# A decoder's mixture-of-experts layer: inputs of six experts by scatter, fetch and transpose, and the first expert started one batch at a time

## The chip, the cores and the metric

The kernel runs on one core of a Trainium2 chip. A core has five engines that run their own instruction queues in order and wait for each other on semaphores: TensorE (PE, matrix products and transposes into PSUM), VectorE (DVE), ScalarE (ACT), GpSimd (POOL) and SyncE (SP, which here only issues DMAs; ACT and POOL issue some too). The metric is the device time of one execution in microseconds; the time before is the median of three runs.

## The reference

The input x is 2 batches of 1024 tokens of 256 features, in fp32. Six sublayers are added to it in turn, each on a layer norm of x: a linear attention with a feed-forward, a cross attention of text to x, a recurrent cell, a causal attention, a cross attention of x to 2 x 64 text rows with 16 heads, and last a mixture of 8 experts. The last two are what matters here:

```python
x = inputs.reshape(G, S, Mm)                       # 8 groups of 256 tokens, 256 features
logits = jnp.einsum('GSM,ME->GSE', x, router_w)    # 8 experts
dispatch, combine = _gating_top2(logits, C)        # two experts a token, C = 64 places per group and expert
expert_inputs = jnp.einsum('GSEC,GSM->EGCM', dispatch, x)
layer_w0 = jnp.einsum('EGCM,EMH->EGCH', expert_inputs, w0_kernel)   # H = 1368
layer_w1 = jnp.einsum('EGCM,EMH->EGCH', expert_inputs, w1_kernel)
hidden = jax.nn.gelu(layer_w0, approximate=True) * layer_w1
expert_outputs = jnp.einsum('EGCH,EHM->EGCM', hidden, wo_kernel)
out = jnp.einsum('EGCM,GSEC->GSM', expert_outputs, combine)
```

A token whose place in an expert is 64 or more is dropped there. `dispatch` is 0 or 1, so `expert_inputs` only moves rows of x to places; a place that no token has is a row of zeros.

## The kernel before

Tokens lie in SBUF as 16 tiles of 128 rows (tile t holds tokens 128t to 128t+127 of both batches in turn; two tiles are one group, four tiles are one *unit*, eight one batch). The layers run one after the other. The part that concerns us begins with the second cross attention, class `Cross`. It works on four units; each step is a small function (`norm`, `turn`, `proj`, `max`, `red`, `sc`, `exp`, `val`, `out`, `add` and so on), and the order of all steps of all units is written out by hand in the string `CROSS_ORDER` (line 1465). A step's name is followed by its unit and, for some, a half. `Cross.run` goes through the string and issues each step's instructions, so that each engine's queue has that order. Steps that begin with `route_` are pieces of `Experts.scores`: the layer norm of a unit into `xn` (L1928 to L183), the transpose by products with the identity (L1945), the router product (L1953). `choose` are the pieces of `Experts.choose`: for one batch, from the router's scores to two slots and two gates for each token; the place in the expert is a running count, made by products with a triangular matrix and with ones (L1992 to L2000). A slot is a row number of a table of expert rows: 512 (`AWAY`) + 512 per expert + the place, with 64 rows per group; 0 if the token was dropped. Units 0 to 2 and the choosing of batch 0 are in `CROSS_ORDER`. PSUM there is three banks of two (`s`) and two single ones (`t`).

`Experts.run_in` follows with two `s`, two `t` and two `o` banks. It has no order by hand at first; a scheduler places the instructions by their dependencies and by program order. Unit 3's scores and batch 1's choosing come first. Then the *dispatch*: for each tile, `dispatch` makes a one-hot matrix of 128 tokens x 512 places (8 experts x 64) with two DVE instructions (L2041, L2042); four such tiles were made in `CROSS_ORDER` (`ones`). PE multiplies it with the token rows (L2089), two tiles into one group, which gives the expert inputs with features on the partitions, as the next product needs them. ACT (L2098) and DVE (L2102) copy them to SBUF for all experts and groups.

Then the experts, one after the other. `hidden` has 11 chunks of up to 128 of the 1368 hidden features (`HCH`): four products of 512 columns for the two weights (L2149), gelu on ACT (L2157), a product on DVE (L2158). `outputs` has 44 products (matmuls) of 256 columns (L2164). Each fp32 matmul shows in the trace as two instructions. The rows of the first six experts (`MOST`) go to the table `eo_rows` in DRAM, on ACT's queue. After expert 5, `gather` fetches for each tile its two rows by an indirect DMA on POOL's queue (L2182, 32 of them) and adds them to x (L2176), while PE works on experts 6 and 7, whose outputs stay in SBUF and come back to the tokens by one product (`combine` makes its matrices, `last` applies them, L2195). Weights are loaded on SP's queue: `load(e + 2)` for w0 and w1 after expert e, with two buffers, and `load_out(e)` for the second weight, with one.

`Experts.constants` runs before the cross attention: number patterns by POOL, and zero rows into three parts of `eo_rows` on SP's queue. The weights' pool `wts`, in which `xn` lies, is closed by `held.close()` before the experts.

## Time and profile before

| what | value |
|---|---|
| median of three runs | 1771.98 us (1766.24 to 1774.56) |
| the profiled execution's own time | 1776.51 us |
| its span, first to last instruction | 1774.4 us |
| PE, DVE, ACT, POOL busy | 1677.3, 804.1, 512.7, 265.7 us |
| mean granted TensorE clock | 0.964 of full |
| first text product of the second cross attention | starts at 1158.37 us |
| end of its last output product (L1811) | 1257.98 us |
| first product of expert 0 | starts at 1305.69 us |
| one expert | 38.04 us hidden, 19.01 us outputs |
| dispatch products L2089 | 64 instructions, 30.7 us busy |
| expert weights to SBUF | 7.1 us from issue to landing, median |

How to read it: times in the trace are counted from the span's start. "Idle before" is time in which an engine did nothing ahead of an instruction, with what released it. The mean duration of a PE instruction overlaps its neighbours, so a run of them is best read from the starts. The granted clock is the share of TensorE's full clock that the throttle let through in a stretch of time.

### The profile page before, as it was taken

How to read it: one execution, taken by the hardware profiler on the slowest of the kernel's cores; microseconds unless marked ns; L12 is line 12 of the kernel's file. 1: busy time of each engine (PE TensorE's matmuls, PEld its weight loads, DVE VectorE, ACT ScalarE, POOL GpSimd, SP SyncE). 2: the span in 40 equal slices, each digit the busy share in tenths (PEclk: the TensorE clock that was granted, in tenths of full speed). 3: DMA queues.
4: the chain of work that ended last, by engine and by line, in shares of the span. 5: the costliest groups of instructions: out<-in, count | busy, mean ns of one | idle time of the engine just before them, and what ended most of it. 6: DMA issues, size and time to landing. Idle time of an engine off the chain costs nothing. (4 is left out here: it accounts for less than half of the span.)

```text
span 1774.4 us, 20965 instructions
## 1 busy us (share of the span) xinstructions
PE 1677.3 (95%) x8686; PEld 882.8 (50%) x8686; DVE 804.1 (45%) x1470; ACT 512.7 (29%) x870; POOL 265.7 (15%) x298
## 2 busy tenths in 40 slices
PE   6889899999999799989999999989899999999998
PEld 4655455343343446543433443456546645665566
DVE  5532224845653524467566667366641131111222
ACT  1221232233324132325555445533121111111110
POOL 2010131133213300203111111220000000000420
PEclk9889999999999899969999999999899999999999
DMA  5000000000000100000000000050003122322321
GB/s 225 1 3 1 0 1 4 1 0 1 1 1 1 36 1 0 31 1 1 1 1 1 1 1 1 1 195 2 1 0 107 69 74 71 107 92 81 100 68 48
DMA packets 30550, 59.16 MB, mean 33 GB/s; under 512 B 3640, under 2 KB 23672, under 8 KB 30072
## 3 DMA queue, kind: packets, MB, share of 16 engines
q1 hardware_dynamic: 25512, 50.46, 8.2%
q0 software_dynamic: 1536, 4.20, 0.9%
q10 hardware_dynamic: 3408, 3.17, 0.5%
q8 instruction: 69, 1.13, 0.3%
q14 instruction: 25, 0.20, 0.0%
HBM read 51.00 MB, written 6.82 MB: 33 GB/s over the span
## 5 line engine op out<-in xcount | busy, mean ns | idle before, releaser
L2149 PE MATMUL ps_s<-pair,w 128*128 128x512 f32 (+1 forms) x704 | 304.8, 592 | 0.2 <-ACT pair L2098 0.2
L2149 PEld LDWEIGHTS ps_s<-pair,w 128*128 128x128 f32 (+1 forms) x704 | 130.9, 187 | 164.4 <-issue 163.3
L1338 ACT ACTIVATE pT<-ps_t 128x512 f32<-128x512 f32 (+3 forms) x344 | 150.6, 490 | 149.5 <-PE ps_t L1303 147.7
L1228 PE MATMUL ps_s<-kT,qT 32*128 32x512 f32 (+3 forms) x768 | 182.1, 571 | 10.3 <-DVE part L1244 6.4
L1303 PE MATMUL ps_t<-qT,kT 32*128 32x512 f32 (+3 forms) x688 | 184.3, 554 | 2.2 <-ACT pT L1338 2.2
L2158 DVE TENSOR_TENSOR hid<-ga,ps_s 128x512 f32<-128x512 f32 (+1 forms) x88 | 60.5, 687 | 272.8 <-ACT ga L2157 272.8
L2164 PE MATMUL ps_o<-wo,hid 128*128 128x256 f32 (+1 forms) x704 | 153.5, 379 | 0.0
L1244 DVE TENSOR_REDUCE part<-ps_s 128x2 f32<-128x1024 f32 (+3 forms) x128 | 130.5, 1024 | 45.4 <-PE ps_t L1303 37.3
L2164 PEld LDWEIGHTS ps_o<-wo,hid 128*128 128x128 f32 (+1 forms) x704 | 133.8, 190 | 22.0 <-issue 4.1
L2157 ACT ACTIVATE ga<-ps_s 128x512 f32<-128x512 f32 (+1 forms) x88 | 52.5, 597 | 246.5 <-PE ps_s L2149 246.5
L1228 PEld LDWEIGHTS ps_s<-kT,qT 32*128 32x128 f32 x768 | 61.4, 194 | 86.8 <-issue 46.6
L1268 PE MATMUL ps_o<-pT,vr 128*32 128x256 f32 (+4 forms) x1408 | 99.5, 361 | 1.8 <-POOL pT L1296 1.5
L1296 POOL TENSOR_SCALAR_AFFINE_SELECT pT<-pT 128x256 f32<-128x256 f32 x128 | 51.9, 407 | 319.4 <-ACT pT L1338 310.3
L910 ACT ACTIVATE pT<-ps_s 128x1024 f32<-128x1024 f32 x64 | 65.5, 1023 | 115.4 <-PE ps_s L903 115.4
L2182 POOL DMA_INDIRECT found<-eo_rows,index x32 | 31.9, 997 | 422.5 <-DMA eo_rows<-rows 387.9
L798 DVE TENSOR_REDUCE part<-ps_s 128x2 f32<-128x1024 f32 x64 | 76.4, 1218 | 28.4 <-PE ps_s L791 27.7
L1236 DVE TENSOR_TENSOR ps_s<-ps_s,causal 128x256 f32<-128x256 f32 x128 | 54.9, 429 | 66.5 <-PE ps_t L1303 44.5
L915 POOL TENSOR_TENSOR acc<-acc,pT 128x1024 f32<-128x1024 f32 x24 | 59.4, 2476 | 160.0 <-ACT pT L910 157.3
L1268 PEld LDWEIGHTS ps_o<-pT,vr 128*32 128x32 f32 x1408 | 28.9, 109 | 98.4 <-issue 84.5
L1303 PEld LDWEIGHTS ps_t<-qT,kT 32*128 32x128 f32 x688 | 71.3, 191 | 12.1 <-ACT pT L1338 6.9
L791 PE MATMUL ps_s<-kT,qT 64*128 64x512 f32 x256 | 72.4, 646 | 0.6 <-DVE part L781 0.6
L830 PE MATMUL ps_o<-pT,vr 128*64 128x512 f32 x256 | 69.5, 624 | 0.0
(381 smaller groups left out, 2272.6 us busy)
## 6 DMA issues: line engine op xcount, KB each, us to landing
w<-in_w SPq DMA_DIRECT2D x32, 684.0 KB, 7.1
wo<-in_wo SPq DMA_DIRECT2D x8, 1280.0 KB, 6.9
eo_rows<-rows ACTq DMA_DIRECT2D x12, 256.0 KB, 4.5
w_ffn<-in_w_ffn SPq DMA_DIRECT2D x1, 2304.0 KB, 15.2
x<-in_x SPq DMA_DIRECT2D x4, 512.0 KB, 4.9
w<-in_w_cell SPq DMA_DIRECT2D x2, 1024.0 KB, 16.8
out_x<-x SPq DMA_DIRECT2D x8, 256.0 KB, 2.2
w<-in_w_lat SPq DMA_DIRECT2D x2, 768.0 KB, 16.8
```

Of the source, the lines that this page charges most:

```text
L791: nc.tensor.matmul(s3[:, hh, :], lhsT=q[rows, qt * P : (qt + 1) * P], rhs=kt[rows, half * 512 : (half + 1) * 512], start=True, stop=True,)
L798: nc.vector.tensor_reduce(part[:, half, qt, :], s3, AX.X, ALU.max, negate=True)
L830: nc.tensor.matmul(self.o[hh * 64 : hh * 64 + 64, :], lhsT=self.vr[b][:, kk, h * 64 : (h + 1) * 64], rhs=pT[:, hh, :], start=first, stop=last,
L910: nc.scalar.activation(pT, s3, AF.Exp)
L1228: nc.tensor.matmul(s3[:, hh, :n], lhsT=q[rows, qt * P : (qt + 1) * P], rhs=kt[rows, at : at + n], start=True, stop=True,)
L1244: nc.vector.tensor_reduce(out, s3[:, :, :n], AX.X, ALU.max, negate=True)
L1268: nc.tensor.matmul(self.o[hh * 32 : hh * 32 + 32, cols], lhsT=vr[:, kk, 4 * grp + hh, :], rhs=pts[hh // 2][:, hh % 2, cols], start=first, ...
L1303: nc.tensor.matmul(out, lhsT=kt[rows, kk * P : (kk + 1) * P], rhs=q[rows, j * 512 + q0 : (j + 1) * 512], start=True, stop=True,)
L1338: nc.scalar.activation(pT[:, hh, q0:], heads[hh][:, q0:], AF.Exp)
L2149: nc.tensor.matmul(s[:n, i * 512 : (i + 1) * 512], lhsT=wt[:, kc, at : at + n], rhs=v[:, kc, :], start=(kc == 0), stop=(kc == DC - 1),)
L2158: nc.vector.tensor_mul(hid[:n, hc, :], ga[:n], s[:n, 512:])
L2164: self.k.nc.tensor.matmul(o, lhsT=hid[:n, hc, st * P : (st + 1) * P], rhs=to[:n, hc, :], start=(hc == 0), stop=(hc == len(HCH) - 1),)
```

## The change

Experts 0 and 1 still get their inputs from PE, in one-hot matrices of 2 x 64 = 128 columns (`ones`, `disp`, `put`). The inputs of experts 2 to 7 are moved by DMA. `scatter` makes row numbers (a dropped token's slot 0 becomes a row of its own, its partition number) and issues 32 indirect DMAs on POOL's queue: each takes the 128 normalised rows of one tile to one of eight tables `xi_rows` in DRAM, one per group. `fetch(e)` reads expert e's places back with eight DMAs on POOL's queue, 64 rows each; `turned(e)` transposes them on PE (8 transposes) and copies them out on ACT. The tables are filled with zeros by eight more DMAs on SP's queue in `constants`; the zeros are the start of `xin`, the input buffer of experts 0 and 1.

Expert 0's hidden chunks are made in two halves, of 256 columns (one batch) each. `CROSS_ORDER` is a new order of the steps, and it now has all eight one-hots of batch 0, its two `disp` and two `put`. A second order by hand, `FIRST_ORDER`, lists what follows: expert 0's 11 chunks for batch 0 (`up`, `gelu`, `mul`, with the chunk as a hexadecimal digit), unit 3's scores, batch 1's choosing, one-hots and dispatch. After that come the scatter, batch 1's chunks of expert 0, and the fetches of experts 2 and 3. In the loop over experts, `turned(e + 1)` and `fetch(e + 3)` stand between the hidden chunks and the outputs. The pools are laid out anew: `wts` stays open to the end.

The core of the diff (the new orders shortened):

```diff
@@ CROSS_ORDER
-sum_3 ones_1 yT_2 val_3 inv_3 ones_3 spr_3 os_3 yT_3 out_2 ones_2 ones_0 out_3 add_2 route_stat_20
-route_stat_21 route_mean_2 route_root_2 add_3 route_norm_21 route_norm_20 route_turn_2 route_xT_2
-route_prod_2 route_copy_2
...
+choose_0 inv_2 spr_2 choose_0 val_2 choose_0 os_2 yT_2 choose_0 sc_30 choose_0 out_2 exp_30 ones_03
+ones_02 ones_01 ones_00 disp_00 add_2 route_stat_20 sum_3 put_00 ones_07 ones_06 ones_05 val_3 inv_3
+ones_04 spr_3 os_3 route_stat_21 disp_01 yT_3 route_mean_2 put_01 out_3 route_root_2 route_norm_20
+route_norm_21 add_3 route_turn_2 route_xT_2 route_prod_2 route_copy_2
@@
+FIRST_ORDER = """
+up_06 route_stat_30 up_08 gelu_06 route_stat_31 route_mean_3 mul_06 route_root_3 gelu_08 mul_08 up_04
+route_norm_30 route_norm_31 route_turn_3 gelu_04 mul_04 route_xT_3 route_prod_3 up_01 route_copy_3
+choose_1 choose_1 choose_1 gelu_01 choose_1 up_00 choose_1 mul_01 choose_1 gelu_00 mul_00 up_0a choose_1
+choose_1 up_05 gelu_0a ones_12 ones_13 up_07 gelu_05 ones_10 ones_11 mul_0a gelu_07 disp_10 mul_07
+mul_05 up_02 put_10 ones_15 ones_16 ones_14 up_09 gelu_02 ones_17 mul_02 disp_11 gelu_09 mul_09 up_03
+put_11 gelu_03 mul_03
+"""
@@ class Experts
-        self.iota = tile("iota", [P, E * C])
+        self.iota = tile("iota", [P, 2 * C])
+        self.iota1 = tile("iota1", [P, 2 * C])
...
+        self.xin = tile("xin", [P, 2, DC, G, C])
...
-        zero = tile("zero", [P, D])
+        zero = self.xin.rearrange("p e m g c -> p (e m g c)")[:, :D]
...
+        self.rows_in = [self.scratch.tile([AWAY + E * ROOM, D], F32, name=f"xi_rows{g}") for g in range(G)]
+        for g in range(G):
+            nc.sync.dma_start(
+                out=self.slots_of(g)[:, 2:, :], in_=zero[:C].unsqueeze(1).to_broadcast([C, E - 2, D])
+            )
...
-    def dispatch(self, t):
-        dm = self.pool.tile([P, E * C], F32, tag="dm", bufs=4, name="dm")
+    def ones(self, b, i):
+        nc, t = self.k.nc, b * TB + i
+        dm = self.ready[t] = self.pool.tile([P, 2 * C], F32, tag="dm", bufs=4, name="dm")
         s1, s2 = (slot[:, t : t + 1] for slot in self.slots)
         nc.vector.tensor_single_scalar(dm, self.iota, s1, op=ALU.is_equal)
         nc.vector.scalar_tensor_tensor(dm, self.iota, s2, dm, ALU.is_equal, ALU.add)
+    def disp(self, b, h):
+        tb = self.placed = self.k.t()
+        for g in range(2):
+            for mc in range(DC):
+                at = (g * DC + mc) * 2 * C
+                for half in range(2):
+                    t = b * TB + 4 * h + 2 * g + half
+                    self.k.nc.tensor.matmul(
+                        tb[:, at : at + 2 * C], lhsT=self.xn[:, t, mc * P : (mc + 1) * P], rhs=self.ready[t],
+                        start=(half == 0), stop=(half == 1),
+                    )
...
+    def scatter(self, pool):
...
+        for half in range(2):
+            for i in range(2):
+                for g in range(G):
+                    t = 2 * g + half
+                    nc.gpsimd.indirect_dma_start(
+                        self.rows_in[g], bass.IndirectOffsetOnAxis(ap=rows[i][:, t : t + 1], axis=0),
+                        self.xn[:, t, :], None,
+                    )
+    def fetch(self, e):
+        if e >= E:
+            return
+        xr = self.fetched[e] = self.hp.tile([P, G // 2, D], F32, tag="xr", bufs=2, name="xr")
+        for g in range(G):
+            h = g % 2 ^ (e == E - 1)
+            self.k.nc.gpsimd.dma_start(out=xr[h * C : (h + 1) * C, g // 2, :], in_=self.slots_of(g)[:, e, :])
+    def turned(self, e):
+        k, xr = self.k, self.fetched.pop(e)
+        s = k.s()
+        for kc in range(DC):
+            for i in range(4):
+                at = (kc * 4 + i) * P
+                k.nc.tensor.transpose(s[:, at : at + P], xr[:, i, kc * P : (kc + 1) * P], k.ident)
+        v = self.inputs[e] = self.hp.tile([P, DC, 512], F32, tag="xe", bufs=2, name="xe")
+        k.nc.scalar.copy(v, s.rearrange("p (c n) -> p c n", c=DC))
...
-    def run_in(self, pool, out, held):
...
+                    self.scatter(pool)
+                    for hc in range(len(HCH)):
+                        self.hidden(0, hc, 4 * C, 4 * C)
+                    self.fetch(2)
+                    self.fetch(3)
             for e in range(MOST):
-                for hid, to in hidden(e):
-                    pass
+                if e:
+                    self.begin(e)
+                    for hc in range(len(HCH)):
+                        self.hidden(e, hc)
+                if e:
+                    self.turned(e + 1)
+                    self.fetch(e + 3)
                 for sp in range(2):
```

For expert 7 the same `turned` stands after expert 6's hidden chunks.

## The prediction

> **What bounds the kernel now.** I read the busy times and the chain that ended last first, then the stretch that the change touches: as windows, as a piece of the chain, and on PE's own timeline.

> ```profile
> PE 1677.3 (95%) x8686; PEld 882.8 (50%) x8686; DVE 804.1 (45%) x1470; ACT 512.7 (29%) x870; POOL 265.7 (15%) x298
> PE 32%; DVE 2%; ACT 0%; issue 0%; POOL 0%; POOLq 0%; DVEq 0%; ACTq 0%
> ```

> TensorE (PE) is busy 95% of the span and carries the chain as far back as it is followed. So a saving is either PE work taken away or a PE gap filled. The windows, split at the end of the last cross-attention output product (1257.98), at the first product of expert 0 (1305.69), and at the ends of its two products (columns: length, busy time of PE, PEld, DVE, ACT, POOL, granted clock, DMA share, GB/s):

> ```profile
> 1158.37:1257.98 99.61, 90.34 (x985) 60.13 (x983) 70.96 (x168) 32.33 (x37) 13.61 (x9) 0.97 0.24 87
> 1257.98:1305.69 47.71, 40.80 (x130) 22.60 (x130) 28.51 (x92) 9.51 (x28) 1.87 (x2) 0.86 0.00 1
> 1305.69:1343.73 38.04, 38.03 (x89) 16.72 (x90) 8.49 (x18) 7.76 (x13) 0.00 (x0) 1.00 0.02 4
> 1343.73:1362.74 19.01, 19.01 (x90) 16.71 (x89) 1.38 (x2) 0.59 (x1) 0.00 (x0) 1.00 0.41 154
> ```

> The experts (rows three and four) are dense at full clock: there only work counts. Cross attention has 9.3 us of PE idle (99.61 - 90.34), the routing stretch 6.9 us, at a clock of 0.86. Its chain:

> ```profile
> 1258.00 1.22 DVE x L1821
> ...
> 1262.44 3.59 PE ps_t L1953 x16
> ...
> 1266.11 1.41 DVE r_st L1928 x4
> ...
> 1268.27 1.02 POOL rs_y L144
> ...
> 1269.87 0.45 PE ps_s L1945
> ...
> 1284.55 20.70 PE ps_s L2089 x48
> ...
> 1305.69 38.04 PE ps_s L2149 x88
> 1343.73 19.01 PE ps_o L2164 x88
> ```

> The reader is to see two things. PE waits up to 1269.87 on a chain of small steps (sum, statistics, root, normalisation); and then 48 dispatch instructions take 20.70 us, 0.431 us each, with nothing else to do. The trace shows two instructions per fp32 matmul.

> **The change, part by part**, against the profiled execution's own time (span 1774.4, 1776.5 with what lies around it; the median of the runs is 1772.0, 4.5 below, and I carry the difference over to the median).

> *Dispatch products narrowed.* Removed: 64 instructions of 512 columns, 64 x 0.431 = 27.6 us of PE, all on the path. Put in: 64 of 128 columns. By width that is 0.108 each; the routing product L1953 (8 columns) runs 16 in 1.88 us, 0.117 each, so the weight load is the floor: 64 x 0.117 = 7.5. **-20.1 us.** One-hot tiles fall on DVE from 16 x (0.475 + 0.749) to 16 x 2 x 0.337 (row of the 128x128 form), 19.6 to 10.8 us; the copies out fall from 24 ACT and 16 DVE to 8 ACT. Both engines have room, so this is worth nothing by itself but shortens the routing chain.

> *Transposes added.* Six experts x 8 of 128x128; L1945 runs 8 in 1.65 us: 6 x 1.65 = **+9.9 us**, all on PE, which has no gap there. Their copy (1.01 us on ACT, row of xT) lies under the 19.01 us of output products; their PSUM bank was released one 3.45 us step of products earlier (gelu 0.60 + product 0.69 after it): no wait. On PE the output products queue behind them; a late transfer would hold up those, and with them everything.

> *Expert 0 in two halves.* 88 instructions of 512 columns become 176 of 256: L2164 runs 88 of 256 in 19.01, 0.216 each, so 38.0 as before. Cost 0. But 11 steps of 1.73 us (19 us) now lie beside the routing.

> *Routing stretch.* I walk the new order with these rows' durations, T0 = end of the last cross output product, in us after T0. PE: transposes of tile group 2 to 1.7, copy awaited to 2.7, routing product to 4.6, two expert steps to 8.1. DVE: the statistics of group 3 (they wait, as L1928 does now, on the previous routing product, 4.6) to 6.1, root to 8.1, 7 combine pieces of 0.3 that stand in DVE's queue and two hidden products to 10.2, normalisation to 11.6. PE: third step to 10.3, **gap 1.3**, transposes to 13.3, **gap 1.1** (copy), routing product 16.5, steps and choosing to 25.5, **gap 1.6** (a PSUM bank freed by a product queued behind four one-hots), then steps and both dispatches to 38. Two extra activation-table loads (1.28 each on ACT) lie in it, one ahead of the exponential: 0.2 late. Then 11 steps of the second half: 57. Before: 1343.73 - 1257.98 = 85.75. Of the 28.75 less, 23.9 is dispatch (27.6 go, and of the new 7.5 half is left here, half now lies before T0); 4.9 is gaps and slow clock.

> *Clock.* PE does not always run at full rate after gaps:

> ```profile
> 1208.45 3.72 PE L1811 MATMUL ps_s<-w,yT 128*128 128x256 f32 x16
> 1217.92 5.38 PE L1811 MATMUL ps_s<-w,yT 128*128 128x256 f32 x16 [0.67 <-DVE yT L1803]
> ```

> The same 16 instructions cost 1.66 us more after gaps of 0.88 and 0.67. [...] by the row each cluster costs about 1.7. I take the row, once: 58.7, **-27.0** for the stretch. [...]

> *Cross attention reordered*, with two of the four dispatches and eight one-hots in it. The same walk from the first text product gives 103.5 against 99.6, that is 3.9 more, of which 3.8 are the two dispatches; but it has no slow clock, where now the clock of 0.97 costs 3 us, and a walk with no slack is about as much too slow. Bounds: +1 (dips gone) to +7 (dips on top). I take **+5**.

> *Scatter and fetch.* 32 indirect writes and 48 plain reads on POOL's queue, none in the trace of before. The nearest row is the gather at the end, issue after issue:

> ```profile
> 1657.17 1.20 POOL L2182 DMA_INDIRECT found<-eo_rows,index  x1 [387.90 <-DMA eo_rows<-rows]
> 1658.68 0.95 POOL L2182 DMA_INDIRECT found<-eo_rows,index  x1 [0.30 <-issue]
> 1659.93 0.95 POOL L2182 DMA_INDIRECT found<-eo_rows,index  x1 [0.30 <-issue]
> ```

> 1.25 us apart, 2.9 to landing, beside DVE's hidden products. Each scatter into one group's rows waits for the one eight issues (10 us) before: landed. The row numbers exist at T0 + 39; 32 scatters and the 8 reads of expert 2 make 40 x 1.25 + 2.9 = 53, ready at T0 + 92. Expert 2's transposes come after expert 0 (58.7), its outputs (19.0) and expert 1's products (38.0): T0 + 116. Slack 24 us, cost 0; from (116 - 39 - 2.9) / 40 = 1.85 us per issue it costs. [...] By the row, nothing. DVE's work there (hidden products with one operand in PSUM) is what ran beside the gather, so I take the row. Lower bound 0 too; no gain is possible here. Later reads have a whole expert (57 us) for 10 us of issues, and are ahead of the gather on POOL.

> *SP's queue* gets eight zero fills (3.1 MB) behind the expert weights, ahead of expert 0's second weights. The DMA engines are now busy to about 1183 at 365 GB/s; 8.6 us more is an estimate from that rate. The first writer of the memory that they read comes some 60 us later. Cost 0.

> **Sum.** Stretch -27.0, cross +5, transposes +9.9: **-12.1 us**. By the other account: dispatch -20.1, transposes +9.9, gaps and clock -2. Predicted median: 1772 - 12 = **1760**.

> **Rivals.**
> - *The gaps close* (22%). The 19 us of expert steps fill every wait, and the front-loaded normalisations of the cross stage leave it without dips: cross +1, stretch at its pure work of 31.6 + 19 + 2 = 53: -33. With +9.9: -22, **1750**. For it: a stretch with more PE work than chain. Against it: two PSUM banks, and DVE is in order.
> - *DVE keeps the routing late* (17%). One-hots, combine pieces and hidden products are in one queue; three waits more of 2 us and one more dip, and the cross stage at +7: -2, **1770**. For it: DVE is busy 71 of 99.6 us in the cross stage.
> - *POOL's transfers are late*, the slower side (8%). Place: PE before the transposes of expert 2. Price: 40 times what an issue exceeds 1.85 us. At 2.15 us it has eaten the gain; at 2.5 it is **1786**. Against it: the row above.
> - *The narrowing isn't worth it*: if 128 columns cost the 0.206 of a transpose per instruction, 64 x 0.206 = 13.2, gain 14.4 only: 1766. The 0.117 row speaks against that.

> **How the numbers follow.** The likeliest case (50%) is 1760, its own range 1752 to 1767 (cross +1 to +7, no or two dips, narrowing at 0.107 to 0.206). "Gaps close" reaches down to 1743. Leaving out the lower third of that (7%) and, above, POOL's 8% and a few per cent of the late routing gives 1745 to 1771. About 0.5% (8.9 us) is what a measurement can tell from no change: faster means below 1763.1. Four fifths of the likeliest case and all of the first rival: 0.40 + 0.22, with a little of the rest 0.64. Slower: POOL 0.08 and 0.05 for an order that comes out worse: 0.13. Same: 0.23.

> **What would show it.** Dispatch: 64 PE instructions near 0.12 us in place of 0.43. Transposes: six groups of 8 in 1.65 us, with no wait on a DMA before them. Routing stretch: from the last cross output to the end of expert 0's hidden products about 59 us. Cross stage: about 105 from the first text product. POOL: scatters 1.25 apart, the first reads landed some 20 us before their use. It is wrong if PE waits for the read rows, if scatters come over 1.85 apart, or if the cross stage changes by more than its bounds.

## The result, and the profile after

The changed kernel took 1758.73 us, the median of 7 runs (1752.07 to 1761.13), beside 1774.02 for the kernel before (7 runs, 1766.24 to 1776.52). The ratio is 0.9917, with a 95% interval of 0.9897 to 0.9937. The forecast was 1760, in a range from 1745 to 1771.

The profiled execution has a span of 1756.9 us, 17.5 less than before. PE is still busy 95% of the span and carries most of the chain (84% of what is followed).

```profile
PE 1661.2 (95%) x8815; PEld 896.8 (51%) x8822; DVE 797.4 (45%) x1471; ACT 519.1 (30%) x873; POOL 321.1 (18%) x380
PE 84%; DVE 11%; ACT 2%; POOL 1%; issue 1%; DMA 0%; SPq 0%; ACTq 0%; POOLq 0%; DVEq 0%
```

The changed kernel's windows are split at the end of the last cross output product (1261.71, T0), at the long row of expert 0's second half (1300.82), at the end of the hidden products of expert 0 (1321.71) and close to the end of its outputs (columns: length, busy time of PE, PEld, DVE, ACT, POOL, granted clock, DMA share, GB/s):

```profile
1155.54:1261.71 106.17, 95.31 (x1019) 62.58 (x1018) 75.21 (x180) 34.13 (x41) 14.54 (x9) 0.95 0.34 111
1261.71:1300.82 39.11, 36.42 (x180) 31.20 (x179) 19.57 (x74) 10.97 (x20) 1.01 (x1) 0.83 0.00 1
1300.82:1321.71 20.89, 20.89 (x99) 18.15 (x98) 5.58 (x17) 4.86 (x13) 13.35 (x14) 1.00 0.20 81
1321.71:1340.44 18.73, 18.73 (x86) 16.16 (x86) 1.11 (x2) 0.93 (x2) 14.16 (x16) 1.00 0.73 265
```

The second row is where the routing now lies beside expert 0: 2.7 us of PE idle (39.11 - 36.42) where there were 6.9, but a granted clock of only 0.83. Put beside the same boundaries of before:

| stretch | before | after | difference | predicted |
|---|---|---|---|---|
| start to the first text product | 1158.37 | 1155.54 | -2.8 | 0 |
| cross attention, to T0 | 99.6 | 106.2 | +6.6 | +5 |
| T0 to the end of expert 0's hidden products | 85.8 | 60.0 | -25.8 | -27.0 |
| from there to the end | 430.7 | 435.2 | +4.5 | +9.9 |
| span | 1774.4 | 1756.9 | -17.5 | -12.1 |

The first row has the same instructions in both kernels. It is not the change: in the profiles below it lies between 1149.0 and 1159.9 us. Before has 105.8 us at half clock ahead of it, after 102.4; the mean granted clock of the whole profile is 0.964 in both, and 0.974 in the two with the shortest start (e7_tail and e4_turn_twice).

PE's own timeline of the changed kernel shows the third row from the inside (columns: start, length from first start to last end, then the line, the tiles and the number of instructions; in brackets the wait ahead and what ended it):

```profile
1261.55 1.04 PE L1975 MATMUL ps_s<-ident,w 128*128 128x128 f32 x8
1263.68 1.95 PE L1983 MATMUL ps_t<-router,xT 128*128 128x8 f32 x16 [1.10 <-ACT xT L1978]
1265.49 7.42 PE L2239 MATMUL ps_s<-xin,w 128*128 128x256 f32 x24
1272.75 1.12 PE L1975 MATMUL ps_s<-ident,w 128*128 128x128 f32 x8
1275.06 2.29 PE L1983 MATMUL ps_t<-router,xT 128*128 128x8 f32 x16 [1.19 <-ACT xT L1978]
1277.20 3.76 PE L2239 MATMUL ps_s<-xin,w 128*128 128x256 f32 x8
...
1290.58 1.03 PE L2266 MATMUL ps_o<-wo,hid 128*128 128x256 f32 x4
1291.97 1.99 PE L2239 MATMUL ps_s<-xin,w 128*128 128x256 f32 x8 [0.36 <-DVE hid L2254]
...
1299.04 1.95 PE L2082 MATMUL ps_t<-dm,w 128*128 128x128 f32 x16
1300.82 20.89 PE L2239 MATMUL ps_s<-xin,w 128*128 128x256 f32 x96
```

Three waits are left, 1.10, 1.19 and 0.36. The same eight products take 1.99 us at 1291.97 and 3.76 at 1277.20: the second lies at a granted clock of 0.50. A dispatch of 16 narrow instructions takes 1.95 us, 0.12 each, where 48 wide ones took 20.70.

The line at 1290.58 isn't in the order written by hand: four of expert 0's 88 output instructions run there already, ahead of a wait. They are about 0.87 us of work that the last row of the table no longer has, so this row shows less than the transposes cost. In the profile the output products behind each of the six groups of 8 transposes begin 0.87 us after the first transpose (1377.45 to 1378.33 for expert 2), 5.2 us in all.

The two new kinds of PE work, as groups (columns: count, busy time and mean ns of one, which overlaps its neighbours):

```profile
L2082 PE MATMUL ps_t<-dm,w 128*128 128x128 f32 x64 | 7.9, 277 | 0.0
L2131 PE MATMUL ps_s<-ident,xr 128*128 128x128 f32 x48 | 6.2, 272 | 0.0
```

And POOL's timeline:

```profile
1304.40 1.24 POOL L2109 DMA_INDIRECT xi_rows<-w,row  x1 [35.51 <-DVE away L2101]
1305.94 0.96 POOL L2109 DMA_INDIRECT xi_rows<-w,row  x1 [0.30 <-issue]
...
1343.89 0.96 POOL L2109 DMA_INDIRECT xi_rows<-w,row  x1 [0.30 <-issue]
1344.85 2.19 POOL L2122 DMA_DIRECT2D xr<-xi_rows  x4
1347.83 0.52 POOL L2122 DMA_DIRECT2D xr<-xi_rows  x1 [0.79 <-DMA xi_rows<-w,row]
1348.86 5.63 POOL L2122 DMA_DIRECT2D xr<-xi_rows  x11 [0.51 <-DMA xi_rows<-w,row]
```

The 32 scatters are 1.27 us apart. Expert 2's eight reads are issued by about 1350.4 (three more after 1348.86, 0.51 each); its transposes start at 1377.5 and no wait stands ahead of them.

### The profile page after: what moved, and what is told of

Same layout as the page of the kernel before. It is cut to its first block, busy times and chain, and to the rows that moved or that the text cites. A ratio compares the mean times of both kernels' runs of the same rounds, so it can differ in the third digit from the quotient of the medians.

```text
span 1756.9 us, 21349 instructions
## 1 busy us (share of the span) xinstructions
PE 1661.2 (95%) x8815; PEld 896.8 (51%) x8822; DVE 797.4 (45%) x1471; ACT 519.1 (30%) x873; POOL 321.1 (18%) x380
## 4 chain that ended last, share of the span: by engine, by line
PE 84%; DVE 11%; ACT 2%; POOL 1%; issue 1%; DMA 0%; SPq 0%; ACTq 0%; POOLq 0%; DVEq 0%
PE ps_s L2239 17%; PE ps_o L2266 9%; PE ps_s L1228 8%; PE ps_o L1268 4%; PE ps_s L903 4%; PE ps_t L1041 4%; PE ps_t L441 3%; PE ps_t L1187 3%; PE ps_o L830 3%; PE ps_f L427 3%; PE ps_s L791 2%; PE ps_t L1303 2%; PE ps_s L705 2%; DVE part L798 1%; PE ps_s L308 1%
## 5 line engine op out<-in xcount | busy, mean ns | idle before, releaser
L2239 PE MATMUL ps_s<-xe,w 128*128 128x512 f32 (+1 forms) x528 | 229.0, 592 | 0.0
L1228 PE MATMUL ps_s<-kT,qT 32*128 32x512 f32 (+3 forms) x768 | 182.0, 571 | 10.3 <-DVE part L1244 6.4
L2254 DVE TENSOR_TENSOR hid<-ga,ps_s 128x512 f32<-128x512 f32 (+2 forms) x99 | 62.0, 627 | 268.7 <-ACT ga L2250 268.6
L2239 PEld LDWEIGHTS ps_s<-xe,w 128*128 128x128 f32 (+1 forms) x528 | 97.9, 187 | 121.3 <-issue 120.0
L1244 DVE TENSOR_REDUCE part<-ps_s 128x2 f32<-128x1024 f32 (+3 forms) x128 | 130.5, 1024 | 45.4 <-PE ps_t L1303 37.3
L2250 ACT ACTIVATE ga<-ps_s 128x512 f32<-128x512 f32 (+2 forms) x99 | 54.4, 549 | 248.0 <-PE ps_s L2239 248.0
L2239 PE MATMUL ps_s<-xin,w 128*128 128x256 f32 (+3 forms) x264 | 83.0, 476 | 0.4 <-DVE hid L2254 0.4
L1303 PEld LDWEIGHTS ps_t<-qT,kT 32*128 32x128 f32 x688 | 71.3, 191 | 12.1 <-ACT pT L1338 6.9
```

The lines of the kernel that those rows point to most:

```text
L1228: nc.tensor.matmul(s3[:, hh, :n], lhsT=q[rows, qt * P : (qt + 1) * P], rhs=kt[rows, at : at + n], start=True, stop=True,)
L1244: nc.vector.tensor_reduce(out, s3[:, :, :n], AX.X, ALU.max, negate=True)
L1303: nc.tensor.matmul(out, lhsT=kt[rows, kk * P : (kk + 1) * P], rhs=q[rows, j * 512 + q0 : (j + 1) * 512], start=True, stop=True,)
L2239: self.k.nc.tensor.matmul(s[:m, i * 512 : i * 512 + n], lhsT=wt[:, kc, at : at + m], rhs=self.inputs[e][:, kc, first : first + n], start=( ...
```

## The experiments

All were run beside the kernel before (medians 1774.13, 1774.76 and 1774.54 in the three sets). Ratios are to it. Three stretches are read from each profile, with the same boundaries as above; "half clock" is the time at a granted clock of 0.50, in cross attention and T0 stretch together, and in the T0 stretch alone. The three stretches come from one profile each and leave the start out, which moves the medians by chance.

| kernel | median us (runs) | ratio, 95% interval | cross | T0 stretch | rest | half clock, both / T0 |
|---|---|---|---|---|---|---|
| before | 1774.0 (7) | 1 | 99.6 | 85.8 | 430.7 | 20.5 / 13.7 |
| after | 1758.7 (7) | 0.9917, 0.9897 to 0.9937 | 106.2 | 60.0 | 435.2 | 23.9 / 13.7 |
| e5_before_narrow | 1765.7 (8) | 0.9955, 0.9942 to 0.9968 | 99.6 | 76.9 | 430.5 | 37.6 / 30.7 |
| e2_no_overlap | 1767.0 (14) | 0.9965, 0.9956 to 0.9974 | 107.9 | 67.3 | 435.4 | 37.5 / 23.9 |
| e1_old_cross | 1754.7 (4) | 0.9893, 0.9870 to 0.9916 | 102.6 | 59.7 | 435.3 | 13.7 / 6.8 |
| e6_fill_waits | 1757.2 (6) | 0.9912, 0.9894 to 0.9929 | 105.7 | 57.7 | 435.2 | 17.1 / 6.8 |
| e3_scatter_twice | 1776.3 (12) | 1.0010, 1.0002 to 1.0019 | 106.2 | 60.0 | 451.3 | 23.9 / 13.7 |
| e4_turn_twice | 1760.8 (4) | 0.9930, 0.9911 to 0.9950 | 106.3 | 56.8 | 440.5 | 17.1 / 6.8 |
| e7_tail | 1757.1 (6) | 0.9900, 0.9879 to 0.9921 | 100.9 | 62.5 | 435.2 | 20.5 / 13.7 |
| e9_both | 1752.2 (4) | 0.9882, 0.9863 to 0.9900 | 100.8 | 57.9 | 435.3 | 10.2 / 3.4 |
| e10_keep_busy | 1755.4 (5) | 0.9902, 0.9884 to 0.9920 | 106.2 | 55.2 | 435.2 | 13.7 / 3.4 |
| e11_best | 1752.2 (5) | 0.9884, 0.9865 to 0.9902 | 100.7 | 56.1 | 435.3 | 10.2 / 3.4 |

**The narrow dispatch alone (e5_before_narrow).** In the kernel before, the one-hots and the dispatch products are cut to 128 columns. The copies keep their sizes and read these columns for every pair of experts, so the inputs of experts 2 to 7 are left out:

```diff
-        dm = self.pool.tile([P, E * C], F32, tag="dm", bufs=4, name="dm")
+        dm = self.pool.tile([P, 2 * C], F32, tag="dm", bufs=4, name="dm")
...
-                            s[:, mc * 512 : (mc + 1) * 512],
+                            s[:, mc * 512 : mc * 512 + 2 * C],
```

> The kernel before with dispatch one-hots and products of 128 columns in place of 512; the copies take the same 128 columns for all four pairs of experts, so the inputs of experts 2 to 7 are left out (they get those of experts 0 and 1). The prediction's step: 64 instructions from 0.431 to 0.117 us, 20.1 us less. If a narrow product costs 0.206: 14.4 less. If DVE's one-hots (0.62 us a tile, 12 tiles after the choosing) become the bound of the last 48 instructions (5.6 us of PE): about 17 less, with PE waits on dm.

Measured: 8.4 us less by the medians, 8.9 less in the T0 stretch. None of the three expectations holds. Two rows of e5's windows, and two lines of its PE timeline, show where the rest went:

```profile
1256.54:1295.41 38.87, 28.06 (x133) 25.70 (x132) 21.30 (x95) 9.44 (x28) 1.89 (x2) 0.60 0.00 1
1295.41:1333.44 38.03, 38.03 (x89) 16.75 (x90) 8.45 (x17) 7.75 (x13) 0.00 (x0) 1.00 0.02 4
```

```profile
1288.41 4.80 PE L2089 MATMUL ps_s<-dm,w 128*128 128x128 f32 x24 [1.93 <-DVE dm L2042]
1293.82 1.13 PE L2089 MATMUL ps_s<-dm,w 128*128 128x128 f32 x8 [0.61 <-DVE dm L2042]
```

In the routing row PE's busy time fell from 40.80 to 28.06, that is by 12.7 and not by 20, while its idle time rose from 6.9 to 10.8. The granted clock fell from 0.86 to 0.60: PE was at half clock for 30.7 us instead of 13.7. So the wide products had done something that the prediction didn't count: they lay over DVE's one-hots, which PE now waits for. And the clock, which in the kernel before was full again at 1275.9, while wide products ran, stayed at half until 1291.6. Why it stayed is not shown; no run separates it from the waits.

**Routing first, expert 0 behind it (e2_no_overlap).** The changed kernel, with all routing steps of its second order ahead of expert 0's steps:

```diff
-up_06 route_stat_30 up_08 gelu_06 route_stat_31 route_mean_3 mul_06 ...
+route_stat_30 route_stat_31 route_mean_3 ... put_11 up_06 gelu_06 mul_06 up_08 ...
```

> The changed kernel with all of unit 3's scores, batch 1's choosing, one-hots and dispatch ahead of the first expert step: nothing of expert 0 lies beside the routing. Theory (the overlap is worth what PE waits in the chain): the chain alone takes about 30 us after the last cross output product, then 22 expert steps of 1.73, so 68 and with one or two clock dips 70 to 72, against 60.1 in the changed kernel: 10 to 12 us longer. Rival (DVE is in order and holds the chain back by as much as the overlap gives): 4 us longer at most.

Measured: 8.3 us more than the changed kernel by the medians; 7.3 more in the T0 stretch, with 23.9 us at half clock there. The first expectation is nearer than the rival; it was a few us too much. The work beside the routing is worth 7 to 8 us. The T0 stretch also has 10.2 us more at half clock here than in the changed kernel, and no run says how much of the 7 to 8 is the clock.

**The old order of cross attention (e1_old_cross).** The order of before, with the one-hots, dispatches and copies of batch 0 set into its last steps:

```diff
-ones_04 spr_3 os_3 route_stat_21 disp_01 yT_3 route_mean_2 put_01 out_3 route_root_2 ...
+... yT_3 disp_00 out_2 put_00 ones_07 ones_06 ones_05 ones_04 disp_01 out_3 put_01 add_2 route_stat_20 ...
```

> The changed kernel with the cross stage's order of before; only the eight one-hots, the two dispatches and two copies of batch 0 are set into its tail. In the changed kernel the cross stage, first text product to last output product, took 106.0 us where it took 99.6 before; the two dispatches explain 3.8. Theory (the new order itself gives nothing, its early gaps and clock dips cost the other 2.6): the stage falls to about 103.4, the total by about 2.6 us against the changed kernel. Rival (the new order is needed to fit the one-hots in): the stage stays at 106 or more and the total is the same or longer.

Measured: 4.0 us less than the changed kernel. Cross attention is 3.6 us shorter, with one window of half clock fewer. The T0 stretch is the same within 0.3 us: it has 6.8 us less at half clock, but PE is idle in it for 5.1 us, against 2.7. So the new order of cross attention cost time, more than was expected of it. Two lines of the changed kernel's timeline are where it begins:

```profile
1166.47 1.64 PE L1688 MATMUL ps_s<-keys,q 32*128 32x128 f32 x32 [2.19 <-ACT q L1680]
...
1171.11 3.42 PE L1666 MATMUL ps_s<-xT,w 128*128 128x512 f32 x4 [1.10 <-ACT xT L1661]
```

In the old order the first of these waits is 1.31 us and the second isn't there. The waits of PE in the stretch add up to 10.8 us in the new order and 8.7 in the old.

**Waits filled with work (e6_fill_waits).** A dispatch and an expert step are moved on PE into the waits of 1.10 and 1.19 us:

```diff
-... route_stat_21 disp_01 yT_3 ... route_turn_2 route_xT_2 route_prod_2
+... route_stat_21 yT_3 ... route_turn_2 disp_01 route_xT_2 put_01 route_prod_2
...
-route_turn_3 gelu_04 mul_04 route_xT_3 route_prod_3 up_01
+route_turn_3 gelu_04 mul_04 up_01 route_xT_3 route_prod_3
```

> The changed kernel with two PE waits filled: the second dispatch of batch 0 moves behind unit 2's routing transposes and one expert step behind unit 3's, each where PE waits 1.1 to 1.2 us for the copy of the transposed rows. In the changed kernel these gaps are followed by runs at about half rate (8 expert instructions of 256 columns in 3.76 us in place of 1.73). If only the gaps go: 2.3 us less. If short gaps cause the dips, as the prediction's row says: the gaps and about 5 us of slow clock go, the stretch falls from 60.1 to about 53 and the total by 6 to 8 us.

Measured: 1.5 us less, a smaller gain than either expectation. (The second dispatch moved into the T0 stretch, so the two stretches must be taken together: 163.4 us against 166.2, with 6.8 less at half clock.) Both waits went, and two others came where the moved work had been: 1.20 us ahead of the last output product (on DVE's `yT`) and 1.56 ahead of the first choosing product (on DVE's mask).

**The dispatch moved in the old order (e7_tail).** As e1, with the second dispatch behind the last output product, and the add of group 3 behind DVE's normalisations:

```diff
-... ones_04 disp_01 out_3 put_01 add_2 ... route_root_2 add_3 route_norm_21 route_norm_20 route_turn_2
+... ones_04 out_3 add_2 ... route_root_2 route_norm_21 route_norm_20 disp_01 add_3 put_01 route_turn_2
```

> The changed kernel with the old order of the cross-attention steps (as in e1_old_cross), its second dispatch moved from between the last two output products to the wait ahead of the transposes of group 2, and the add of group 3 put behind the normalisations on VectorE. Theory (a wait of TensorE costs its own length and, in addition, whole windows of about 3.4 us at half clock, of which dense products pay half): against e1_old_cross the wait of 1.73 us goes and with it one or two half-clock windows of the two that follow: 1754.7 - 1.7 - 1.7 to 3.4 = 1749.6 to 1751.3. Rival (half-clock windows come from the small instructions, not from the waits): only the wait, 1753. Second rival (the wait is only moved, since the normalisation starts no earlier): 1754.7.

Measured: 1757.1, with runs from 1749.0 to 1759.7. All three expectations lie below the median. The wait of 1.73 us did go: cross attention and T0 stretch, which must be taken together since the dispatch moved from the one to the other, are 163.5 against 162.4 in e1, but with 6.8 us more at half clock. The theory that a wait taken away takes its half-clock windows with it failed here.

**Both (e9_both).** e7 and three steps of expert 0 moved in the second order, with the gelu and product of the first:

```diff
-route_turn_3 gelu_04 mul_04 route_xT_3 route_prod_3 up_01 route_copy_3 choose_1 choose_1 choose_1 gelu_01 choose_1 up_00 ...
+route_turn_3 gelu_04 mul_04 up_01 route_xT_3 gelu_01 mul_01 route_prod_3 up_00 route_copy_3 choose_1 choose_1 choose_1 choose_1 up_0a ...
```

> e7_tail, with three steps of expert 0 moved on TensorE as well: one into the wait for the copy of group 3's transposes, one into the wait for the first choosing step, one behind it, with the gelu and product of the first of them ahead of the choosing. Theory (waits and the half-clock windows after them): 1.2 to 1.6 us less waiting than e7_tail and no half-clock window left behind the second routing product: 1747 to 1750. Rival (VectorE and ScalarE, in order, then delay the choosing by what is put ahead of it): no better than e7_tail.

Measured: 1752.2, 4.8 less than e7, and 2 above the range expected. No window of half clock is left behind the second routing product, as expected. A wait further on grew from 0.36 us in the changed kernel to 1.98: PE now gets there earlier, while DVE's hidden product still stands behind four one-hots (line numbers are one higher in this kernel):

```profile
1285.28 1.99 PE L2240 MATMUL ps_s<-xin,w 128*128 128x256 f32 x8 [1.98 <-DVE hid L2255]
```

**Scatters twice (e3_scatter_twice).**

```diff
-        for half in range(2):
+        for half in (0, 1, 0, 1):
```

> The changed kernel with each of the 32 scatter writes issued twice in a row: 32 x 1.265 us = 40.5 us more on POOL's queue, and nothing more on TensorE. Theory (POOL's transfers are hidden by a slack of about 20 us, as the trace of the changed kernel shows it): TensorE waits some 20 us ahead of expert 2's transposes and the time is about 1758.7 + 20 = 1779. Rival (the slack is much larger, because the order of the transfers doesn't bind): no change, 1759. [...]

Measured: 1776.3, 17.5 us more. PE's timeline:

```profile
1394.06 1.30 PE L2131 MATMUL ps_s<-ident,xr 128*128 128x128 f32 x3 [12.09 <-DMA xr<-xi_rows]
1396.30 1.30 PE L2131 MATMUL ps_s<-ident,xr 128*128 128x128 f32 x5 [0.94 <-DMA xr<-xi_rows]
1397.39 20.59 PE L2266 MATMUL ps_o<-wo,hid 128*128 128x256 f32 x88
```

PE waits 13.0 us for the rows read back, and what follows is slow for a moment: the 88 outputs take 20.59 us instead of 19.0. The mean granted clock of this profile is 0.959, against 0.964 in the changed kernel's. The 64 scatters stay 1.27 us apart. So 40.5 us more of POOL cost 13.0 of waiting: the slack in the changed kernel is 27.5 us. The place and the kind of the price are as the rival of the prediction had them, and the slack is wide enough that it doesn't decide here.

**Transposes twice (e4_turn_twice).**

```diff
-        for kc in range(DC):
+        for kc in (0, 1, 0, 1):
```

> The changed kernel with the 48 transposes of the inputs read back done twice into the same place: 48 more instruction pairs of 128 columns on TensorE in the dense part. By the row that the prediction used (8 in 1.65 us): +9.9, 1768.6. By the trace of the changed kernel (8 in about 0.9 to 1.0 us): +5 to +6, 1764. Rival (they lie in waits and cost nothing): 1759.

Measured: the rest behind expert 0's hidden products is 440.5 against 435.2, 5.3 more, 0.11 us for each of the 48. The median is only 2.1 above the changed kernel's, inside what the two medians' own spread allows. This kernel has the changed kernel's instructions up to the end of expert 0's hidden products, and yet its T0 stretch is 56.8 us instead of 60.0. Windows of 3.41 us, laid so that they begin where the clock changes, show why. First the changed kernel:

```profile
1273.01:1276.42 3.41, 2.22 (x21) 1.92 (x18) 0.46 (x2) 1.33 (x2) 0.00 (x0) 1.00 0.00 0
1276.42:1279.84 3.42, 3.42 (x12) 2.95 (x12) 1.71 (x8) 1.73 (x3) 0.00 (x0) 0.50 0.00 0
1279.84:1283.25 3.41, 3.41 (x14) 3.14 (x13) 1.23 (x7) 1.67 (x2) 0.00 (x0) 0.50 0.01 2
1283.25:1286.66 3.41, 3.41 (x11) 2.71 (x9) 0.73 (x5) 0.05 (x1) 0.00 (x0) 0.50 0.00 0
1286.66:1290.08 3.42, 3.42 (x19) 2.85 (x19) 2.81 (x15) 0.71 (x2) 0.00 (x0) 1.00 0.00 0
```

and the same place in e4_turn_twice:

```profile
1267.17:1270.59 3.42, 2.23 (x20) 2.02 (x19) 0.42 (x1) 1.15 (x2) 0.00 (x0) 1.00 0.00 0
1270.59:1274.00 3.41, 3.41 (x12) 2.87 (x12) 1.85 (x9) 1.73 (x3) 0.00 (x0) 0.50 0.00 0
1274.00:1277.41 3.41, 3.41 (x24) 3.15 (x22) 1.61 (x8) 1.67 (x2) 0.00 (x0) 1.00 0.01 2
```

The same work is followed by three windows at half clock in the one and by one in the other. The windows lie 0.2 us differently against the work: the expert step behind the second routing product starts 0.78 us into the window (at 1277.20) in the changed kernel, and 0.60 us into it (at 1271.19) here.

**Useless work in the waits (e10_keep_busy).**

```diff
         t = k.t()
+        if u > 1:
+            spare = self.xn[:, 0:2, :].rearrange("p t d -> p (t d)")
+            nc.tensor.matmul(t, lhsT=k.ident, rhs=spare, start=True, stop=True)
```

> The changed kernel with one product more, of 512 columns and of no use, ahead of each of the routing products of groups 2 and 3, into the bank that they then overwrite: it needs nothing that TensorE would wait for, and falls into the two waits of 1.10 and 1.19 us for the copies (2 instructions of 0.43 us each, 0.86). Theory (it is the waits that bring windows of half clock): the work added lies in the waits and costs nothing, and of the 13.7 us at half clock behind the last output product of the changed kernel at most 3.4 are left; dense products cost half of the rest, so about -5: 1753.5. Rival (half clock comes with stretches of small instructions, waits or not): no less time at half clock, 1759. Second rival (the product delays the path by what doesn't fit in): 1760.

Measured: 1755.4, 3.4 less than the changed kernel with two products more. The T0 stretch is 55.2, 4.8 less, and 3.4 us at half clock are left there:

```profile
1264.32:1267.74 3.42, 3.18 (x22) 2.48 (x21) 0.66 (x3) 1.00 (x2) 0.00 (x0) 1.00 0.03 5
1267.74:1271.15 3.41, 3.41 (x10) 2.69 (x9) 3.25 (x16) 0.95 (x1) 1.09 (x1) 0.50 0.00 0
...
1274.56:1277.98 3.42, 3.09 (x22) 2.25 (x21) 0.42 (x1) 1.25 (x2) 0.00 (x0) 1.00 0.00 0
1277.98:1281.39 3.41, 3.41 (x24) 3.12 (x24) 2.06 (x10) 2.72 (x4) 0.00 (x0) 1.00 0.00 0
```

Both sides of the question are in these rows. The window with 0.33 us of idle (3.09 busy) is followed by full clock; the one with 0.24 of idle (3.18 busy) by half clock. Idle time alone doesn't decide it. The e4 rows say that a part of what was gained here could have come by the place of the windows; all five runs (1754.2 to 1756.2) lie below six of the seven runs of the changed kernel.

**All together (e11_best).** e9, with the useless product ahead of the first of the two routing products, and the hidden product ahead of the one-hots:

```diff
-choose_1 up_05 gelu_0a ones_12 ones_13 up_07 gelu_05 ones_10 ones_11 mul_0a gelu_07
+choose_1 up_05 gelu_0a mul_0a ones_12 ones_13 up_07 gelu_05 ones_10 ones_11 gelu_07
```

> e9_both with two edits more: the product of no use ahead of the routing product of group 2 only (as in e10_keep_busy), and the hidden product of VectorE that e9_both's TensorE waited 1.98 us for put ahead of the four one-hots. Theory: the last window of half clock behind the last output product (3.4 us in e9_both) goes, worth 1.7, and of the wait about 1.4 go: 1752.2 - 3.1 = 1749. Rival (the one-hots are then 0.4 us late, their dispatch waits instead, and half clock stays): 1752.

Measured: 1752.2, the same as e9. In the profile the wait of 1.98 us went and the T0 stretch is 1.9 shorter, but the median doesn't show it, and the half-clock window behind the first routing product stayed, as the rival had it. e9 and e11 are the fastest kernels of this study, 6.5 us below the changed one by the medians; their intervals and that of the changed kernel just overlap.

## Why the prediction was right, point by point

- *Dispatch narrowed, -20.1.* The size of an instruction was right: 16 in 1.95 us, 0.12 each, not the 0.206 of a transpose, so the rival "not worth it" falls. The weight loads of these 16 run without a gap, for 1.97 us at 1293.58; those of the routing product's 16, of 8 columns, take 1.86 of its 1.95 us. But "all on the path" was wrong. Taken alone, the narrowing gave 8.4 (e5): behind the wide products lay DVE's one-hots and the recovery of the clock. The second account, "dispatch -20.1, gaps and clock -2", puts the gain in the wrong place. Of the 25.8 us that the T0 stretch lost, the narrowing alone has 8.9 (e5) and the work beside the routing 7.3 (e2 against after); of the other 9.6 (e5's 76.9 less e2's 67.3), 3.9 are two dispatches that now lie ahead of T0, and the rest go with shorter waits and 6.8 us less at half clock, which no run separates. The sum held because the walk through the new order counted the whole stretch and not the dispatch by itself.
- *Routing stretch, -27.0.* It measured -25.8. The waits were fewer than in the walk: 1.10, 1.19 and 0.36 us, and none ahead of unit 3's transposes, against 1.3, 1.1 and 1.6. The clock cost more: 1.7 was taken, once, and 13.7 us ran at half clock, nearly all of them with PE at work, of which half, 6.8, is lost (an estimate, from the 3.76 us at half clock and 1.99 at full of the same eight products). That the two errors cancel is luck: the walk without any clock loss (57) was about 4 too long, as 60.0 less 6.8 is 53.2, an estimate. e10 has 3.4 us at half clock, and 55.2 less 1.7 gives about the same, 53.5; so does e4, 56.8 less 3.4.
- *Cross attention, +5.* It measured +6.6, inside the bounds of +1 to +7. By e1, 3.0 of it are the two dispatches and what came with them in the old order (predicted 3.8), and 3.6 the new order, for which the prediction had little more than 1.
- *Transposes, +9.9.* This is the term that was mis-sized most: 5.2 by the profile, 0.87 us for each row of 8, and 5.3 for 48 by e4. (The stretch itself grew by only 4.5, since four output instructions had moved out of it.) The row used for it, 8 in 1.65 us, held waits: the trace of before shows, in its timeline of PE's weight loads in that row, that they wait between one another for DVE's normalisation, whose pieces are made at the same time:

```profile
1229.84 0.14 PEld L1945 LDWEIGHTS ps_s<-ident,w 128*128 128x128 f32 x1 [0.18 <-DVE w L183]
...
1230.17 0.53 PEld L1945 LDWEIGHTS ps_s<-ident,w 128*128 128x128 f32 x5 [0.19 <-DVE w L183]
```

  The same eight, six microseconds earlier, start at 1223.13 and are followed by the next instruction at 1224.01: 0.11 each. That row was the one to take, since the rows read back are complete when the transposes begin.
- *Scatter and fetch, 0.* Right. Scatters 1.27 apart (predicted 1.25), row numbers at T0 + 43 (predicted 39), expert 2's transposes at T0 + 116 (predicted 116). e3 puts the slack at 27.5, predicted 24. That POOL's transfers could come late beside DVE's work was the author's estimate, and it was not shown: the 64 scatters of e3 stayed 1.27 us apart, and in the changed kernel DVE's hidden products of 256 columns take 0.42 us beside the scatters, as they do ahead of them.
- *Expert 0 in halves, zero fills, 0.* In the changed kernel 96 instructions of 256 columns take 20.89 us, 0.216 each at full clock, as taken. No wait on a fill or a weight shows in PE's timeline.

The sum was -12.1. The medians differ by 15.3, the spans by 17.5, of which 2.8 are the start. The remaining 2.6 to 3.2 are the transposes and the four outputs that ran early, less what cross attention and the routing stretch took. So the middle of the range was met by a sum whose parts were off by up to 5 us, in both directions.

Of the rivals, "the gaps close" was half right: most of them did, and the clock took it back. What it takes to come near its 1750 is shown by e9 and e11. "DVE keeps the routing late" is what happens in e5, and not in the changed kernel, where expert 0's steps fill the waits.

What is not settled: how a change of order will fall against the windows of the clock. Their place against the work differs from one profile to the next, and in e4, with two windows fewer at half clock than the changed kernel, the T0 stretch was 3.2 us shorter. Filling a wait kept the clock in one place and not in another: in e10 no half clock follows the second routing product, and 3.4 us of it follow the first, as in e11.

## What to carry to other kernels

Before a long instruction row is counted as a gain, look at what lies behind it on the other engines and at the clock: a row that covers DVE's work is worth only what its cover leaves, and the gain is cashed by the work that takes its place. Take a duration from a row at full clock, start to start, and not from one whose parts wait for another engine in between: that nearly doubled a term here. And where the order of a few steps is compared, count the windows of half clock in the profile of each before the orders are judged: one more is worth about 1.7 us on dense products (an estimate, half of its 3.41; two were 3.2 in e4), and it can fall by chance. A wait can be filled with useless work at a gain: in e10 a product of 512 columns in each of two waits left 3.4 us at half clock in the T0 stretch, where the changed kernel has 13.7, and the median was 3.4 us lower.

## What the runs showed of the hardware

A long wait isn't needed ahead of it: the longest wait ahead of a half-clock window of the T0 stretch in the changed kernel was 1.19 us. Nor is a window in which PE is busy always followed by full clock: the one from 1276.42, with PE busy for all of 3.42 us, was followed by two more at half clock. The same instructions, with their place against the windows changed by 0.2 us, took 56.8 or 60.0 us.

The columns that PE streams in a window can be counted in the profiles of the two kernels: each PE instruction's columns are shared out by time, from its start to the start of the next one (or to its own end, if that is earlier). Around T0:

| profile | windows of 3.41 us from | columns of each; in bold those followed by half clock |
|---|---|---|
| before | 1255.44 | 2799, **1024**, **121**, **7**, **1567**, 2074, 2036 |
| after | 1259.37 | 3600, **860**, 2071, 3655, **809**, **1534**, **1096**, 1899, 3626 |

In these sixteen windows half clock followed 7 to 1567 columns and full clock 1899 or more. Elsewhere in the same profiles the count doesn't sort them. In the cross attention of the kernel before, where many products are of 32*128 and 128*32, the windows from 1176.9 and 1214.5 have 4084 and 4134 columns and are followed by half clock; at the start of the changed kernel, up to 14 us, windows with 0, 157 and 1595 columns are followed by full clock. No run varied the columns alone, and what the clock goes by is not shown.
